# A group's score and attention products in stands of six and two, in a kernel ordered by a planner

## The chip, the cores and the metric

The kernel runs on one core of a Trainium2 chip (trn2). The metric is the device time of one execution in microseconds (us), as the median of several runs. A profile is one further execution, recorded by the hardware.

## What is computed

The input x holds 128 items of 128 x 512 floats, adj is one 128 x 128 adjacency matrix. The reference has two layers, cut here to what matters (shapes are of one item):

```python
# layer 0: gnn on adj, then layernorm over the last axis
A = adj @ x;  C = adj @ x + b[:, None]
pre = A[:, None, :] + (C - A)[:, :, None]      # C - A is b alone
x = layernorm(x + max(relu(pre), axis=-1))     # one number for each row: relu(max(A) + b)
# layer 1: masked attention with 8 heads, projection, two layernorms
q, k, v = split(x @ w_qkv, heads=8)
attn = softmax(where(adj == 0, -inf, q @ k.T * 64 ** -0.5))
o = (attn @ v) @ w_proj + b_proj
o = o + layernorm(o) * ln_gamma + ln_beta
x = layernorm(x + o)
```

All is in float32 with the accuracy of float32. A full float32 product takes TensorE several passes, so the kernel splits most operands: a number is written as a high part and a low rest, and a product is the sum of high x high, low x low and a term of the differences, each in the faster type fp32r.

## The kernel before

**Items and groups.** The 128 items are worked in 32 groups of G = 4. In a program place, the first number is the group and the second the item of the group or, for dense products, one of twelve: 0 to 3 are v of the four items, 4 to 11 are the eight slices of q and k for all four items at once.

**Steps of an item.** Each step is a small function that issues one or a few instructions.
- Layer 0: load (DMA of x), conv (adj times x on PE, full float32, L632), cmax (L643), relu, then either bn, ba, rstdx, shiftx (items 0 and 1; bn is L680 on DVE) or add0, sq0, rstd0, shift0 (items 2 and 3), and norm0 on ACT.
- Transposed x: xpl (ACT copies into 16-bit planes, L716), xrow (DMA to rowsx in memory), xcross (a transposing DMA back, xT), then xmask, xsub, xhigh, xd make the three split forms x_h, x_l, x_d.
- Dense products: dm (eight fp32r products, L817 and L818) and dd (four, L823), then main (ACT takes the first bank out of PSUM, L842) and rest (DVE adds the second, L846).
- Attention: S (scores: sixteen products, each with 64 rows of the array, L863), masked and rmax (DVE, L877 and L885), exps (ACT, eight exponentials, L902), recip and wts (DVE, L911), pln (ACT, L917), row (DMA to rows), cross (transposing DMA, eT), AV (weights times v: sixteen products, each with 64 columns of the array, L949).
- Projection: omask, osub, ohigh, od make oh, ol and od (L739, L967, L743 or L745, L749); po and pod are its products (eight and four, again L817, L818, L823; od and o are printed with the item's number); pmain and prest (DVE, L986 and L1012) take them out.
- The end of an item: res, resx, resb, reso bring in the first layer's x a second time; sq1, sm1, st1, n1a, n1b and sq2, sm2, st2, norm2 are the two layernorms; out is the last DMA.

In the last group, T (transposes on PE) and wT take the place of pln, row and cross, and S of item 3 adds the mask by four products (L857).

**The order.** The order on every engine (PE, ACT, DVE, POOL and SP, which issues nearly all DMAs) is written out: each step has a place in a table (STEADY for the middle groups, FIRST for groups 0 and 1, LAST for groups 30 and 31, SETUP for weights and constants), a group's places are shifted by g x PERIOD, all steps are sorted by place, and each engine gets its steps in that order. Places in STEADY read like microseconds; only the order that they give reaches the chip. Each engine runs in order and waits at a step whose inputs or buffer are not ready.

```python
u0 = g * PERIOD
...
at(u, single[kind], b)
...
plan.sort(key=lambda p: p[:2])
```

**Buffers.** HOMES says, for each kind of tile and each group, which numbered buffer it gets. PSUM has two pools: ps_1 with four single banks (pa of conv, pav of AV, pm and pd of dense products, pom and pod of the projection) and ps_2 with two double banks (psc of the scores; pp and ppo, where a product that TWO marks with 1 keeps both its banks together). So TWO's rows dense and po say which products take a double bank. Its rows d and h say which of xd and od (first four entries for x, next four for o) and of xhigh and ohigh run on POOL: a 1 puts the difference on POOL and not on DVE, the high part on POOL and not on ACT.

In the middle groups PE meets the special products of a group in this order, with dense products between the brackets: [AV of items 2 and 1 of the group before, S of 0 and 1], [S of 2 and 3, AV of 3 of the group before], [AV of 0]. Such a run without a dense product in it is called a stand here. The last one stands between conv products.

Of the kernel before, what the change touches and what calls it, by code (L numbers as in the profile page):

```python
# [8 lines left out]
FP = mybir.dt.float32  # L9
# [18 lines left out]
PERIOD = 55.65721  # L28
STEADY = {
    'load': [-84.387, -101.525, -92.757, -104.895],  # L30
    'conv': [-75.113, -75.979, -71.238, -73.133],
    'cmax': [-74.046, -74.912, -70.171, -71.594],
    'relu': [-73.282, None, -69.407],
    'bn': [-79.685, -90.339],
    'ba': [-78.963, -87.311],
    'rstdx': [-71.500],
    'shiftx': [-67.749],
    'add0': [None, None, -69.067, -62.343],
    'sq0': [None, None, -68.228, -60.929],
    'rstd0': [None, None, -60.228],  # L40
    'shift0': [None, None, -20.160],
    'norm0': [-66.552, -60.223, -55.338, -56.756],
    'xpl': [-65.714, -57.708, -54.441, -46.941],
    'xrow': [-64.641, -56.635, -53.368, -45.398],
    'xcross': [-61.931, -52.928, -48.082, -41.718],
    'xmask': [-54.951, -43.405, -41.164, -36.407],
    'xsub': [-48.801, -42.437, -37.819, -35.400],
    'xhigh': [-46.997, -35.315, -37.063, -35.835],
    'xd': [-26.327, -29.608, -22.523, -17.793],
    'dm': [4.837, 11.201, 6.655, 16.122, -27.595, -10.169, -22.140, -32.141, -33.960, -23.959, -25.777, -30.323],  # L50
    'dd': [9.383, 10.292, 20.788, 27.152, -12.896, -6.532, -8.350, -5.623, -4.714, -16.490, -7.441, -11.987],
    'main': [7.711, 13.218, 9.668, 20.862, -11.380, -7.877, -11.865, -20.987, -31.942, -21.472, -23.760, -26.046],
    'rest': [10.516, 14.823, 28.292, 38.461, -10.247, -5.049, -3.873, -4.461, -2.608, -11.977, -6.331, -9.059],
    'S': [0.000, 0.997, 13.110, 14.107],
    'masked': [1.644, 5.106, 15.417, 27.161],
    'rmax': [3.380, 8.064, 24.101, 29.327],
    'exps': [4.623, 15.506, 26.003, 35.155],
    'recip': [10.406, 20.865, 29.217, 43.570],
    'wts': [11.110, 22.861, 30.453, 44.268],
    'pln': [13.703, 24.200, 32.382, 51.803],  # L60
    'row': [20.837, 26.467, 34.304, 55.119],
    'cross': [24.197, 29.995, 47.113, 59.806],
    'AV': [37.158, 54.685, 53.762, 70.756],
    'omask': [41.739, 55.758, 58.432, 77.236],
    'osub': [42.962, 56.693, 64.847, 80.884],
    'ohigh': [46.552, 56.528, 63.853, 84.748],
    'od': [47.794, 58.991, 74.103, 86.254],
    'po': [51.853, 58.675, 73.718, 96.599],
    'pod': [57.646, 64.130, 75.536, 100.236],
    'pmain': [60.163, 63.121, 81.492, 101.655],  # L70
    'prest': [61.894, 65.455, 82.210, 102.843],
    'res': [41.103, 53.159, 76.024, 78.628],
    'resx': [52.598, 58.118, 78.904, 82.973],
    'resb': [53.844, 60.258, 80.456, 101.811],
    'reso': [62.664, 71.516, 83.739, 104.286],
    'sq1': [66.881, 66.175, 85.753, 103.922],
    'sm1': [66.639, 71.226, 88.501, 103.613],
    'st1': [68.723, 67.062, 90.348, 105.534],
    'n1a': [69.485, 72.830, 94.712, 105.600],
    'n1b': [77.841, 75.237, 95.973, 108.029],  # L80
    'sq2': [78.635, 93.900, 96.767, 110.927],
    'sm2': [90.058, 96.472, 97.864, 110.751],
    'st2': [94.366, 98.154, 99.952, 125.624],
    'norm2': [95.548, 105.334, 102.729, 130.428],
    'out': [97.230, 106.460, 109.286, 132.611],
# [3 lines left out]
        'load': [-311.682, -309.097, -309.092, -289.177],  # L89
        'conv': [-301.956, -285.978, -284.699, -252.846],  # L90
        'cmax': [-276.686, -268.417, -252.229, -243.444],
        'relu': [-275.480, -258.624, -245.414, -236.373],
        'bn': [-298.400, -272.353, -260.336, -251.012],
        'ba': [-276.256, -271.589, -254.792, -248.969],
        'rstdx': [-272.599, -269.091, -248.273, -238.464],
        'shiftx': [-269.130, -253.340, -240.209, -232.976],
        'norm0': [-266.978, -249.667, -237.355, -228.662],
        'tx': [-266.046, -245.978, -230.203, -224.006],
        'copy': [-248.555, -225.163],
        'pv': [-226.671, -221.380],  # L100
        'keep': [-210.841, -209.446],
        'xmask': [-237.451, -231.282, -228.825, -220.542],
        'xsub': [-232.807, -226.381, -226.376, -184.540],
        'xhigh': [-235.047, -224.785, -216.680, -210.529],
        'xd': [-232.210, -205.597, -206.130, -125.910],
        'dm': [None, None, 8.596, 7.614, -27.333, -7.643, -16.082, -37.145, -46.738, -6.339, -11.225, -36.934],
        'dd': [None, None, 7.519, 13.277, -25.364, -7.365, -10.388, -25.470, -13.330, -4.235, -16.812, -26.914],
        'main': [None, None, 9.424, 14.292, -8.119, -5.070, -13.376, -26.832, -30.312, -2.548, -8.551, -26.673],
        'rest': [None, None, 11.233, 35.409, -6.802, -0.906, -5.599, -18.911, -0.865, 0.048, -7.653, -11.149],
        'S': [0.071, 3.526, 11.673, 10.965],  # L110
        'masked': [4.362, 7.230, 17.266, 20.450],
        'rmax': [4.711, 7.375, 18.562, 27.402],
        'exps': [6.391, 14.172, 25.847, 36.857],
        'recip': [12.522, 19.013, 30.495, 40.437],
        'wts': [13.400, 26.323, 35.020, 43.252],
        'pln': [14.511, 33.217, 37.332, 48.065],
        'row': [24.078, 40.304, 45.297, 48.373],
        'cross': [31.686, 41.648, 45.892, 58.796],
        'AV': [38.517, 48.815, 50.261, 70.407],
        'omask': [43.804, 51.125, 58.512, 81.275],  # L120
        'osub': [44.138, 53.164, 60.683, 86.080],
        'ohigh': [45.476, 55.853, 65.956, 87.153],
        'od': [52.512, 60.084, 71.048, 87.521],
        'po': [48.135, 56.775, 71.054, 93.215],
        'pod': [54.003, 61.222, 76.700, 97.775],
        'pmain': [55.811, 59.410, 82.388, 98.578],
        'prest': [56.183, 64.180, 82.945, 101.590],
        'res': [46.370, 42.491, 71.387, 79.013],
        'resx': [63.966, 47.589, 79.420, 100.786],
        'resb': [70.459, 70.785, 81.534, 105.046],  # L130
        'reso': [70.474, 72.568, 90.218, 105.110],
        'sq1': [63.146, 65.537, 87.020, 104.749],
        'sm1': [69.929, 71.912, 90.063, 105.360],
        'st1': [72.212, 72.233, 94.751, 105.573],
        'n1a': [78.126, 76.071, 96.130, 106.436],
        'n1b': [82.298, 76.869, 96.351, 108.235],
        'sq2': [82.739, 79.519, 97.605, 111.944],
        'sm2': [87.842, 82.457, 97.845, 117.109],
        'st2': [90.386, 87.300, 99.888, 120.030],
        'norm2': [95.187, 93.693, 107.047, 122.559],  # L140
        'out': [99.205, 96.285, 112.844, 132.585],
    },
    {
        'load': [-131.325, -146.629, -109.252, -117.493],
        'conv': [-103.575, -126.260, -90.173, -103.104],
        'cmax': [-94.745, -125.823, -83.341, -89.398],
        'relu': [-80.440, None, -75.846],
        'bn': [-106.480, -139.224],
        'ba': [-99.960, -134.812],
        'rstdx': [-91.047],  # L150
        'shiftx': [-79.188],
        'add0': [None, None, -74.243, -74.248],
        'sq0': [None, None, -69.318, -69.504],
        'rstd0': [None, None, -68.606],
        'shift0': [None, None, 14.252],
        'norm0': [-78.560, -74.678, -62.455, -54.484],
        'xpl': [-77.724, -72.376, -61.942, -52.495],
        'xrow': [-75.147, -66.114, -52.002, -51.491],
        'xcross': [-52.007, -55.219, -51.696, -50.648],
        'xmask': [-51.097, -51.522, -47.743, -46.741],  # L160
        'xsub': [-47.766, -48.031, -45.293, -45.741],
        'xhigh': [-44.210, -49.814, -42.689, -41.925],
# [31 lines left out]
        'n1b': [80.034, 71.944, 89.870, 107.555],  # L194
        'sq2': [83.515, 87.175, 100.626, 112.358],
        'sm2': [85.095, 77.407, 91.265, 112.382],
        'st2': [89.764, 89.887, 102.645, 129.724],
        'norm2': [94.880, 93.286, 102.685, 130.269],
        'out': [99.098, 100.886, 102.826, 130.308],
    },  # L200
# [951 lines left out]
```

## Time and profile before

| what | us |
|---|---|
| median of three runs | 1847.24 (1846.62 to 1847.33) |
| the profiled execution, its own time | 1842.58 |
| its span, from the first instruction to the last | 1840.6 |
| PE busy | 1804.2 |
| DVE busy | 1548.9 |
| ACT busy | 1541.5 |
| POOL busy | 1311.4 |

The clock that PE was granted is 0.996 of full over the span. A page of the profile gives busy time by engine first, then groups of instructions with their mean duration and what they waited for. In a line of the order of time the columns are: start, duration, engine, line of the kernel, operation, output<-inputs, count of merged instructions, and in brackets the engine's idle time before it and what ended it. A line of the waits has: who waited, for whom, total, times, longest. A line of busy time by stretch has: the stretch, its length, busy time and count of PE, weight loads, DVE, ACT and POOL, granted clock, share of DMA time, GB/s.

### The profile page before, as it was taken

Reading aid. Unit: us, or ns where it says so; the run is one execution under the profiler, and the core shown is the slowest. Engines: PE = TensorE matmul, PEld = TensorE weight load, DVE = VectorE, ACT = ScalarE, POOL = GpSimd, SP = SyncE. Lnnn points to the kernel's source line nnn. Section 1 sums busy time; section 2 is a strip of 40 time slices with the busy share of each in tenths; the row PEclk is TensorE's granted clock in tenths of the full one; section 3 lists DMA queues with packets and bytes.
Section 4 is the critical chain, followed back from the end, with each engine's and each line's share of the span. In section 5 each row is a group of like instructions: output and inputs, shape, how many; then the busy total and the mean of one; then the engine's idle time right before and its main releaser. Section 6 shows DMA issues by size and latency. Waiting matters only on the chain. (4 is left out here: it accounts for less than half of the span.)

```text
span 1840.6 us, 32730 instructions
## 1 busy us (share of the span) xinstructions
PE 1804.2 (98%) x10541; PEld 1426.1 (77%) x10541; DVE 1548.9 (84%) x2584; ACT 1541.5 (84%) x3927; POOL 1311.4 (71%) x1935
## 2 busy tenths in 40 slices
PE   8999999999999999999999999999999999999995
PEld 5777777778777788777787777787777787777874
DVE  7988888888888888888888888888888888788877
ACT  6988888888888888888888888888888888878865
POOL 4277787677777777777676877776877777667768
PEclk9999999999999999999999999999999999999998
DMA  5556665666575676565676656675656665656641
GB/s 150 173 149 182 170 171 162 163 179 183 150 185 165 158 191 171 157 175 160 175 183 166 170 169 162 174 184 161 180 162 159 185 184 149 178 144 178 155 126 46
DMA packets 486139, 302.91 MB, mean 165 GB/s; under 512 B 399440, under 2 KB 403664, under 8 KB 485968
## 3 DMA queue, kind: packets, MB, share of 16 engines
q1 hardware_dynamic: 485104, 299.70, 60.6%
q8 instruction: 84, 1.38, 0.3%
q10 hardware_dynamic: 864, 1.12, 0.2%
q14 instruction: 87, 0.71, 0.1%
HBM read 72.16 MB, written 131.07 MB: 110 GB/s over the span
## 5 line engine op out<-in xcount | busy, mean ns | idle before, releaser
L902 ACT ACTIVATE e<-e,nmax 128x128 f32<-128x128 f32 x1016 | 393.1, 390 | 34.9 <-DVE nmax L885 34.8
L917 ACT COPY planes<-e 128x2048 uint16<-128x2048 uint16 x124 | 234.9, 1894 | 41.7 <-DMA rows<-planes 20.4
L1018 ACT ACTIVATE square<-o,sum 128x512 bf16<-128x512 f32 x256 | 183.6, 717 | 88.0 <-DVE o L1012 87.0
L1002 POOL TENSOR_SCALAR xb<-xb,sum 128x512 f32<-128x512 f32 x128 | 109.5, 855 | 194.9 <-DMA xb<-in_x_dram 185.7
L1024 POOL TENSOR_TENSOR sum<-sum,mhalf 128x1 f32<-128x1 f32 (+1 forms) x287 | 195.5, 681 | 23.9
L1009 POOL TENSOR_TENSOR xb<-xb,o 128x512 f32<-128x512 f32 x125 | 173.4, 1387 | 35.9 <-DVE o L1012 33.7
L902 ACT ACTIVATION_READ_ACCUMULATOR e<-e,nmax 128x1 f32 x1016 | 191.9, 189 | 0.0
L911 DVE TENSOR_TENSOR e<-e,sums 128x1024 f32<-128x1024 f32 x128 | 175.9, 1375 | 0.1
L1005 POOL TENSOR_TENSOR xb<-xb,beta_sb 128x512 f32<-128x512 f32 x128 | 167.4, 1308 | 4.9
L716 ACT COPY xplanes<-xt 128x1024 uint16<-128x1024 uint16 x124 | 129.1, 1041 | 41.4 <-DMA rowsx<-xplanes 40.5
L1023 POOL TENSOR_SCALAR sum<-sum 128x1 f32<-128x1 f32 (+1 forms) x287 | 122.4, 427 | 56.3 <-ACT square L1018 36.9
L877 DVE SCALAR_TENSOR_TENSOR e<-psc,mask 128x1024 f32<-128x1024 f32 x127 | 154.4, 1216 | 1.3 <-PE psc L863 1.3
L885 DVE TENSOR_REDUCE nmax<-e 128x8 f32<-128x1024 f32 x127 | 151.7, 1195 | 0.1
L643 DVE TENSOR_REDUCE rm<-pa 128x1 f32<-128x512 f32 x128 | 87.7, 688 | 68.0 <-PE pa L632 66.4
L739 DVE TENSOR_SCALAR oxh<-pav 128x512 int32<-128x512 int32 x128 | 87.2, 681 | 64.5 <-PE pav L949 62.8
L949 PEld LDWEIGHTS pav<-eT,v 128*64 128x64 f32 x2048 | 109.8, 137 | 38.1 <-issue 16.4
L863 PEld LDWEIGHTS psc<-qkT 64*128 64x128 f32 x2048 | 119.5, 188 | 18.5 <-issue 17.0
L749 POOL TENSOR_TENSOR x_d<-x_h,x_l 128x512 fp32r<-128x512 f32 x97 | 128.9, 1332 | 6.2 <-DVE x_l L755 6.2
L949 PE MATMUL pav<-eT,v 128*64 128x128 f32 x2048 | 133.2, 277 | 0.0
L863 PE MATMUL psc<-qkT 64*128 64x128 f32 x2048 | 132.3, 279 | 0.6 <-DVE v L846 0.4
L632 PE MATMUL pa<-xt,adjT 128*128 128x512 f32 x256 | 131.1, 615 | 0.5 <-DVE adjT L561 0.4
L1039 DVE SCALAR_TENSOR_TENSOR o<-o,sum,gamma_sb 128x512 f32<-128x512 f32 x128 | 99.4, 778 | 31.0 <-POOL xb L1009 23.8
(4288 smaller groups left out, 5533.3 us busy)
## 6 DMA issues: line engine op xcount, KB each, us to landing
rows<-planes SPq DMA_DIRECT2D x124, 512.0 KB, 3.8
xt<-in_x_dram SPq DMA_DIRECT2D x128, 256.0 KB, 3.6
xb<-in_x_dram SPq DMA_DIRECT2D x128, 256.0 KB, 3.0
out_dram<-o SPq DMA_DIRECT2D x128, 256.0 KB, 3.2
rowsx<-xplanes SPq DMA_DIRECT2D x124, 256.0 KB, 2.8
wraw<-in_L_gnn_w_qkv_dram SPq DMA_DIRECT2D x8, 256.0 KB, 3.6
xT<-rowsx SPq DMA_TRANSPOSE x124, 3.6
eT<-rows SPq DMA_TRANSPOSE x124, 4.4
```

The costliest lines, as they stand in the source:

```text
L632: nc.tensor.matmul(pa[b], adjT, xs[b], start=True, stop=True)
L863: nc.tensor.matmul(psc[:, s, hp, :], qkT[hs, hp, i, :], qkT[hs, KC + hp, i, :], start=not with_mask, stop=not with_mask or hp == HP - 1,)
L877: nc.vector.scalar_tensor_tensor(es[b], pscs.pop(b).rearrange("p s a m -> p (s a) m"), scale, mask_b, op0=ALU.mult, op1=ALU.add,)
L885: nc.vector.tensor_reduce(nmaxs[b], es[b], AX.X, ALU.max, negate=True)
L902: nc.scalar.activation(es[b][:, j, :], src[:, j, :], AF.Exp, bias=nmax[:, j : j + 1], scale=by, accum_out=sums[b][:, j : j + 1],)
L911: nc.vector.tensor_tensor(es[b], es[b], sums.pop(b)[:, :, None].to_broadcast([P, H, P]), op=ALU.mult,)
L917: nc.scalar.copy(pl, es.pop(b).rearrange("p h m -> p (h m)").bitcast(U16).rearrange("p (m s) -> p s m", s=2),)
L949: nc.tensor.matmul(pavs[b][s * HD : (s + 1) * HD, hp, :], v[:, h * HD : (h + 1) * HD], eT[:, s * HP + hp, :], start=True, stop=True,)
L1005: nc.gpsimd.tensor_tensor(xbs[b], xbs[b], beta_sb, op=ALU.add)
L1009: engine.tensor_tensor(xbs[b], xbs[b], os[b], op=ALU.add)
L1018: nc.scalar.activation(square, src, AF.Square, bias=s[:, 0:1], scale=-float(D), accum_out=s[:, 1:2],)
L1024: nc.gpsimd.tensor_tensor(s, s, mhalf[:, :n], op=ALU.pow)
```

## The change

All tables are replaced: PERIOD, STEADY, FIRST, LAST, SETUP, TWO and HOMES. In the middle groups, PE's special products now stand as [S of items 2 and 0, AV of items 1 and 0 of the group before, S of 1 and 3] and [AV of 2 and 3 of the group before]; the four conv products stand singly between dense ones. In FIRST, LAST and SETUP many places are thousands, with the order in them alone of effect. Each step still occurs as often as before. TWO moves one high part and one difference of a group to another engine and changes which products use a double bank. There is a new branch in po and pmain (one full float32 product in place of the split ones in the last group) with two new steps, lp and ocopy; TWO's row plain is all zeros and no table holds places for lp or ocopy.

```diff
-PERIOD = 55.65721
+PERIOD = 55.29520
 STEADY = {
-    'load': [-84.387, -101.525, -92.757, -104.895],
+    'load': [-87.861, -88.331, -108.598, -116.436],
...
-    'bn': [-79.685, -90.339],
+    'bn': [-75.588, -84.750],
...
-    'xrow': [-64.641, -56.635, -53.368, -45.398],
-    'xcross': [-61.931, -52.928, -48.082, -41.718],
+    'xrow': [-68.575, -61.581, -56.570, -52.833],
+    'xcross': [-63.957, -56.130, -50.263, -41.238],
...
+    'dm': [-2.906, 7.680, 4.876, 14.911, -28.277, -11.089, -13.817, -31.005, -15.635, -26.459, -32.823, -23.775],
+    'dd': [11.317, 12.226, 20.653, 26.109, -17.453, -11.998, -6.543, -18.363, -9.271, -16.544, -7.452, -8.362],
+    'main': [8.036, 20.173, 9.041, 17.942, -26.260, -9.072, -11.799, -25.069, -12.689, -20.790, -30.806, -20.305],
...
-    'S': [0.000, 0.997, 13.110, 14.107],
-    'masked': [1.644, 5.106, 15.417, 27.161],
+    'S': [0.000, 2.887, -0.997, 3.884],
+    'masked': [1.332, 5.529, 0.201, 14.546],
...
-    'row': [20.837, 26.467, 34.304, 55.119],
-    'cross': [24.197, 29.995, 47.113, 59.806],
-    'AV': [37.158, 54.685, 53.762, 70.756],
+    'row': [15.477, 39.515, 52.228, 59.088],
+    'cross': [23.799, 44.363, 61.747, 64.017],
+    'AV': [57.210, 56.287, 72.115, 73.038],
...
 LAST = {
     -2: {
-        'load': [-107.823, -91.695, -103.440, -73.255],
+        'load': [-91.734, -89.477, -107.242, -114.634],
...
-        'bn': [-105.550, -89.567],
+        'bn': [-84.588, -84.468],
...
     -1: {
-        'AV': [43.664, 48.635, 62.710, 73.994],
+        'AV': [2284.230, 2274.397, 2965.116, 2626.927],
...
 TWO = {
+    'plain': [0, 0, 0, 0],
     'bn': [1, 0],
-    'd': [1, 1, 1, 0, 0, 1, 0, 1],
-    'dense': [1, 0, 0, 0, 1, 0, 1, 0, 0, 0, 0, 0],
-    'h': [1, 0, 0, 0, 0, 1, 0, 0],
-    'po': [0, 0, 1, 0],
+    'd': [0, 1, 0, 1, 1, 1, 1, 1],
+    'dense': [0, 1, 0, 0, 0, 0, 0, 0, 0, 0, 0, 0],
+    'h': [0, 0, 0, 0, 1, 0, 0, 0],
+    'po': [1, 0, 1, 0],
...
+    def plain(b):
+        return bool(TWO["plain"][b % G]) and b >= B - G
...
     def po(b, two):
-        product(("o", b), two)
+        if plain(b):
...
+        else:
+            product(("o", b), two)
```

## The prediction

> **What bounds the kernel now.** I read the page's first part, then busy time by stretch, then the waits of PE, then PE's order of time around the attention products. A difference under 0.2% (3.7 us) can't be told from none here.
>
> ```profile
> PE 1804.2 (98%) x10541; PEld 1426.1 (77%) x10541; DVE 1548.9 (84%) x2584; ACT 1541.5 (84%) x3927; POOL 1311.4 (71%) x1935
> ```
> ```profile
> 500.00:1500.00 1000.00, 999.37 (x5864) 797.18 (x5860) 844.79 (x1418) 860.25 (x2194) 733.54 (x1076) 1.00 0.64 171
> ...
> 1770.00:1841.00 71.00, 49.30 (x336) 37.66 (x331) 54.27 (x89) 40.54 (x120) 57.50 (x87) 0.92 0.21 64
> ```
> ```profile
> PE pd_('o', 109)_17866 L823 <- DVE o L1012: 2.5, 1, 2.5
> PE pd_(31, 3)_20003 L823 <- DVE o L986: 2.4, 1, 2.4
> PE pm_('o', 127)_20090 L818 <- DVE w_l L967: 2.3, 1, 2.3
> PE pd_('o', 127)_20104 L823 <- POOL w_d L749: 2.1, 1, 2.1
> PE pp_(31, 0)_19602 L823 <- ACT v L842: 2.0, 1, 2.0
> ```
> In the middle PE never rests; the others have 14% (ACT) to 27% (POOL) spare. Order matters there only through what PE pays between products. The first score products of neighbouring groups start 55.58 us apart in 17 of the 25 pairs from group 3 to 28; the other eight add 4.2 us in all. The end is different: PE is idle 21.7 of the last 71 us, and waits after 1690 add to 11.0 us.
>
> What PE pays between products is read from start times:
>
> ```profile
> 928.63 0.39 PE L818 MATMUL pm_('o', 60)_10246<-p_l,ol 128*128 128x512 f32 x1
> 928.95 1.97 PE L949 MATMUL pav<-eT,v 128*64 128x128 f32 x32
> 930.84 2.06 PE L863 MATMUL psc<-qkT 64*128 64x128 f32 x32
> 932.83 1.20 PE L823 MATMUL pd_('o', 60)_10322<-p_d,od 128*128 128x512 f32 x4
> 933.86 0.39 PE L817 MATMUL pm_('o', 61)_10334<-p_h,oh 128*128 128x512 f32 x1
> ```
> ```profile
> 910.55 1.88 PE L632 MATMUL pa<-xt,adjT 128*128 128x512 f32 x4
> 912.36 1.09 PE L949 MATMUL pav<-eT,v 128*64 128x128 f32 x16
> 913.38 1.12 PE L632 MATMUL pa<-xt,adjT 128*128 128x512 f32 x2
> 913.94 1.50 PE L823 MATMUL pd_(16, 9)_10106<-x_d,w_d 128*128 128x512 f32 x4
> 915.28 1.02 PE L632 MATMUL pa<-xt,adjT 128*128 128x512 f32 x2
> ```
> A dense product takes 0.227 us from start to start, a pair of AV products 0.109 and a pair of score products 0.112, in a run of their own kind. First fence: 0.32 into AV instead of 0.23 (0.09 too much); two AV batches 1.89 instead of 16 x 0.109 = 1.75 (0.14); two score batches 1.99 instead of 1.79 (0.20); the four dense ones after them 1.03 instead of 0.91 (0.12). So **prices**: 0.21 for a stand (in and out of dense work), 0.20 for each block of scores, 0.15 for each block of AV, whatever their length. Check on the second fence: from 910.55 to 915.28 are 4.73; six passes of conv (0.4285), one AV batch (0.875) and four dense ones (0.907) make 4.35. 0.38 against 0.21 + 0.15.
>
> **What the Trainium skill says.** "TensorEngine Tiling (Array Packing)", Key Properties: changing the tiling mode, not just the tile, drains TensorE. Scores are 64x128, AV 128x64, the rest 128x128. The trace agrees: each change costs 0.09 to 0.2 us. "TensorE: Matmul & The Clock Gate", Architectural detail: ScalarE's and VectorE's queues are strict FIFO, so what waits holds all behind it; the wait at 1607 (below) is that. The same page, Part 1: idleness throttles PE's clock until it has been busy for a window of some 3.4 us. After 2.5 us of idleness at 1608 four products took 1.98 us from first start to last end, against 1.07 in the middle: agrees, a stall costs more than itself.
>
> **The change, part by part.** The order of every engine follows from sorting the tables by place; I sorted both.
>
> *Stands.* Before, per group: [A2 A1 S0 S1], [S2 S3 A3], [A0] between conv products: 3 stands, 2 score blocks, 3 AV blocks: 3 x 0.21 + 2 x 0.20 + 3 x 0.15 = 1.48. After: [S2 S0 A1 A0 S1 S3], [A2 A3]: 2 stands, 2 and 2 blocks: 1.12. So -0.36 a group. Over the program I count 99 stands, 64 score and 97 AV blocks before (48.1 us), 76, 68 and 69 after (39.9): the ends, where the order splits stands, give some back. -8.2 us, all on PE, which sets the end: taken in full. A conv product now stands alone four times a group, not in two runs; entering from dense work starts it 0.232 after instead of 0.227, so +0.007 x 29 more entries = +0.2. Sum **-8.0**. The mode changes inside the new stand (S to AV to S) both occur in the old ones, so no price is unseen.
>
> *Work moved between engines.* Per group one high part (L743, 1.50 on POOL) goes to ACT (L745, 0.62); one difference (L749) goes from DVE (0.68) to POOL (1.30). POOL -0.2, ACT +0.6, DVE -0.7, of 55: hidden under PE while ACT keeps its 14%; if that cover is gone, +0.6 a group. The number of products, exponentials and DMAs is the same.
>
> *DMA leads.* SP issues in order and holds when a source isn't ready; its waits before are mostly transposes issued before their rows landed. Leads of rows to eT were 3.4, 3.5, 12.8, 4.7 us for a median landing of 3.8; now 8.3, 4.9, 9.5, 4.9. rowsx to xT: 2.7 at the least before, 4.6 now (landing 2.8). Better, but AV stands at least 6.7 us after the issue of its eT in both (landing 4.4): no PE time, 0. One lead is tighter: bn of item 1 stands 3.6 us after its load (11.2 before) and a load lands in 3.6 (1 in 20 over 4.8). What is queued behind bn on DVE is the rest step of v; then qkT sums wait, then PE. The table leaves DVE 0.8 us after it. 0 to +0.3 a group; taken: within the next item.
>
> *PSUM slots.* Three of the twelve dense products of a group took a wide slot (dm4 among them), now one; the output products take two instead of one. So 34 single-bank tiles a group pass four banks, 32 before. By the places, the narrowest reuse was 0.4 to 0.7 us before; now dd5 starts 0.69 after main8 starts on the same bank, dm5 0.71 after main6, dd11 0.71 after main5, and main takes 0.58. So 0.04 of margin. ACT's run from main4 to main8 (13.6 us) has almost no gap. Bounds: -4.2 (all present stray waits go, as the DMA leads are better) to +0.8 a group (22). Taken: 0, new small waits for the old ones. S1 and S3 reuse the wide slots of S2 and S0: 1.2 to 1.4 us left after masked; 13 us before; no wait.
>
> *The wait at 1607.* DVE's order of time shows a bn (L680) that waited 3.4 us for its load; prest queued behind it, PE's pd waited for that, then ran slow; that group took 60.4 instead of 55.6: 4.8 us. In the old LAST table this bn stood 2.1 us behind its load. In the new one the leads of bn there are 7.1, 5.0, 12.5 and 22.6. What could be late next is another transfer; I take **-3.5**, bounds -4.8 and +1.
>
> *The last two groups.* 11.0 us of waits after 1690. Old order ends AV, o, q for items 2 and 3 with nothing else left for PE. The new one does T for all, keeps o and q of item 30.3 for the gap after them, and puts both last AV ahead of three output products in a row (8.2 us). Counting by hand after q31.1: DVE needs prest, n1b, osub, omask, reso, n1a, n1b (5.0), ACT a square (0.9), POOL st2 (1.0) before od31.3 (1.3): 8.2, while PE has one AV, o31.0, q31.0, o31.3 (5.8): a wait of 2.4 stays. T31.2 and o31.3 come out even. With 3 to 4 unseen, 6 of 11: -5, bounds -9 and +4. The chain behind the last product (12.1 us now: 1828.5 to 1840.6) gets a POOL step more in it: +0.7. Sum **-4.3**.
>
> *The start.* Waits up to 200 us are some 5 us before (0.2 to 0.7 each). New order: two weight conversions stand ahead of those that d0.8 needs, by hand +1; nothing says that the rest is better. **+1.5**, bounds -4 and +5.
>
> plain is all zeros and no table has places for lp or ocopy: none of that runs, 0.
>
> Sum: -8.0 + 0 - 3.5 - 4.3 + 1.5 = **-14.3**. The profiled execution took 1842.58 (span 1840.6 and 2.0 around it), 4.7 less than the median of 1847.24; against it 1828.3, as a median 1833.
>
> **Rivals.** (1) *Switches alone*: the ends don't gain. For: hand counting sees few queues at once. -7 to -9: 1839. (2) *The ends gain fully*: -9 there, stray waits gone: -21, 1826. (3) *Slower: ACT releases banks late.* At the places with 0.04 us left (dd5, dm5, dd11), PE waits in every group. For: no gap in ACT's run, ACT +0.6; against: ACT's measured steps fit the places within 0.02 us. At 0.8 a group, 28 groups: +22, so 1855; it decides from 14.3 / 28 = 0.5 a group. (4) *No change*: PE's switches are saved, but a wait before the next product takes them up each group: 1847.
>
> **How the numbers follow.** Forecast 0.52 (1828 to 1838), rival 1 0.20, rival 2 0.10, rival 4 0.07, rival 3 0.11. Faster by over 0.2%: 0.82; same 0.07; slower 0.11. The range of 8 in 10 goes from 1824 (inside rival 2) to 1846 (rival 1 with its bounds, the edge of rival 4); the slower case is left out.
>
> **What would show it.** Right: groups 55.2 to 55.3 apart; six-batch stand about 5.9 us from first score to first dense product; no wait of 2 us near 1600; under 8 us of PE waits after 1680. Wrong: PE waits for ACT (L842) at pd or pm of 5, 6, 8, 11 in many groups, groups over 55.6 apart, or DVE waits for xt before L680 in each group.

## The result, and the profile after

The change makes no difference that can be measured: 1847.55 us after against 1847.14 before, medians of twelve runs each, ratio 1.0002 (95% interval 0.9993 to 1.0011). The forecast was 1833, and its range ended at 1846. The profiled execution took 1845.31 us (span 1843.2), 2.7 more than that of before.

First the lines that answer to those of before. The page's busy times of the kernel after:

```profile
PE 1805.7 (98%) x10541; PEld 1426.9 (77%) x10541; DVE 1535.2 (83%) x2551; ACT 1556.9 (84%) x3958; POOL 1293.9 (70%) x1937
```

Busy time by stretch, the middle and the end:

```profile
500.00:1500.00 1000.00, 999.42 (x5890) 796.79 (x5889) 836.38 (x1400) 869.17 (x2213) 718.92 (x1077) 1.00 0.65 170
1770.00:1843.20 73.20, 49.72 (x310) 37.81 (x308) 49.15 (x83) 38.84 (x116) 56.75 (x83) 0.84 0.19 58
```

PE's waits, the longest of the whole kernel:

```profile
PE adjT_ps L554 <- DMA adj_sb<-in_adj_dram: 4.1, 1, 4.1
PE pm_('o', 127)_20094 L813 <- ACT w_h L741: 3.9, 1, 3.9
PE pd_('o', 127)_20104 L819 <- POOL w_d L745: 2.5, 1, 2.5
```

And the new stand of six batches in PE's order of time:

```profile
928.33 0.39 PE L814 MATMUL pm_(16, 0)_10225<-w_l,x_l 128*128 128x512 f32 x1
928.64 2.06 PE L859 MATMUL psc<-qkT 64*128 64x128 f32 x32
930.63 1.97 PE L945 MATMUL pav<-eT,v 128*64 128x128 f32 x32
932.53 2.06 PE L859 MATMUL psc<-qkT 64*128 64x128 f32 x32
934.51 0.50 PE L813 MATMUL pm_(16, 2)_10332<-w_h,x_h 128*128 128x512 f32 x1
934.85 0.40 PE L814 MATMUL pm_(16, 2)_10332<-w_l,x_l 128*128 128x512 f32 x1
```

The engines moved as forecast (ACT up, DVE and POOL down), the 2.5 us wait at the `pd_` of output 109 is gone, and two waits in the last group are the only ones over 1 us that PE has left after the start. The stand takes 5.87 us from first score to first dense product, as forecast. Yet the span is no shorter. Where it went is seen by cutting the span at the first score product of a group:

| stretch, us | before | after | difference |
|---|---|---|---|
| start to group 3 | 205.6 | 203.8 | -1.8 |
| group 3 to group 28 | 1393.7 | 1394.0 | +0.3 |
| group 28 to group 31 | 171.6 | 168.4 | -3.2 |
| group 31 to the end | 69.7 | 77.0 | +7.3 |

In the 25 pairs of the second row the undisturbed step went from 55.58 to 55.75; before, stray waits raised the mean of all 25 to 55.75 too, and after there are almost none (mean 55.76). So two things have to be explained: the step that did not fall to 55.2, and the last 7.3 us.

### The profile page after: what moved, and what is told of

Its sections match the earlier page's. It is cut to its first block, busy times and chain, and to the rows that moved or that the text cites. A ratio compares the mean times of both kernels' runs of the same rounds, so it can differ in the third digit from the quotient of the medians.

```text
span 1843.2 us, 32644 instructions
## 1 busy us (share of the span) xinstructions
PE 1805.7 (98%) x10541; PEld 1426.9 (77%) x10541; DVE 1535.2 (83%) x2551; ACT 1556.9 (84%) x3958; POOL 1293.9 (70%) x1937
## 5 line engine op out<-in xcount | busy, mean ns | idle before, releaser
L745 POOL TENSOR_TENSOR od<-oh,ol 128x512 fp32r<-128x512 f32 x124 | 165.0, 1331 | 133.8 <-DVE ol L963 78.0
L1051 POOL TENSOR_TENSOR sum<-sum,mhalf 128x1 f32<-128x1 f32 (+1 forms) x287 | 213.6, 744 | 23.9
L1036 POOL TENSOR_TENSOR xb<-xb,o 128x512 f32<-128x512 f32 x125 | 163.4, 1307 | 53.4 <-DVE o L1039 50.8
L907 DVE TENSOR_TENSOR e<-e,sums 128x1024 f32<-128x1024 f32 x128 | 161.4, 1261 | 1.1
L739 POOL TENSOR_SCALAR oh<-oxh 128x512 fp32r<-128x512 f32 x31 | 64.0, 2065 | 113.4 <-DVE oxh L735 27.3
L1029 POOL TENSOR_SCALAR xb<-xb,sum 128x512 f32<-128x512 f32 x128 | 119.2, 931 | 17.6 <-DMA xb<-in_x_dram 17.4
L945 PE MATMUL pav<-eT,v 128*64 128x128 f32 x2048 | 127.5, 276 | 1.8 <-DVE e L873 0.9
L1039 DVE SCALAR_TENSOR_TENSOR o<-o,sum,xb 128x512 f32<-128x512 f32 x128 | 100.6, 787 | 20.8 <-POOL sum L1051 15.5
L1087 ACT ACTIVATE o<-o,sum 128x512 f32<-128x512 f32 x128 | 103.2, 807 | 12.3 <-POOL sum L1083 12.2
```

What stands on the lines that cost most here:

```text
L745: engine.tensor_tensor(d, h.bitcast(FP), l.bitcast(FP), op=ALU.subtract)
L907: nc.vector.tensor_tensor(es[b], es[b], sums.pop(b)[:, :, None].to_broadcast([P, H, P]), op=ALU.mult,)
L945: nc.tensor.matmul(pavs[b][s * HD : (s + 1) * HD, hp, :], v[:, h * HD : (h + 1) * HD], eT[:, s * HP + hp, :], start=True, stop=True,)
L1036: engine.tensor_tensor(xbs[b], xbs[b], os[b], op=ALU.add)
L1051: nc.gpsimd.tensor_tensor(s, s, mhalf[:, :n], op=ALU.pow)
```

## The experiments

In the names of steps and items, dd5 is dd of dense product 5, main8 is main of dense product 8, sq21 is sq2 of item 1, and 31.3 is item 3 of group 31 (127 in the names of the profile). Each ratio is to the kernel before on the same chip. "Step" and "end" are read from one profile of each kernel: "step" is the median distance of first scores in the 25 pairs, and "end" the time from the first score of group 31 to the end. Kernels with nearly the same step and end as after have ratios up to 0.0016 apart from it (e4, e6, e9), and the end varies from 76.2 to 77.1 among kernels with one and the same last group (after, e1, e2, e3). What lies under that is not read.

| run | ratio (95%) | step | end |
|---|---|---|---|
| after | 1.0002 (0.9993 to 1.0011) | 55.75 | 77.0 |
| e1_two_scratch | 0.9978 (0.9972 to 0.9985) | 55.51 | 77.1 |
| e2_interleave | 0.9981 (0.9974 to 0.9987) | 55.52 | 76.2 |
| e3_main8 | 0.9976 (0.9969 to 0.9982) | 55.52 | 76.2 |
| e5_scratch_before | 0.9992 (0.9984 to 1.0001) | 55.58 | 69.6 |
| e7_conv | one run | 55.62 | 69.7 |
| e4_tail | 1.0014 (1.0007 to 1.0021) | 55.76 | 77.2 |
| e12_after_o | 1.0005 (0.9997 to 1.0013) | 55.76 | 76.2 |
| e9_pool_relief | 1.0018 (1.0010 to 1.0026) | 55.75 | 78.4 |
| e6_chain | 1.0017 (1.0008 to 1.0025) | 55.75 | 76.5 |
| e8_all | 0.9976 (0.9966 to 0.9986) | 55.49 | 76.6 |
| e10_all_relief | 0.9966 (0.9952 to 0.9980) | 55.49 | 74.7 |
| e11_o_buffers | 0.9952 (0.9940 to 0.9965) | 55.49 | 73.3 |
| e15_last_sums | 0.9955 (0.9941 to 0.9969) | 55.49 | 71.3 |

### The middle groups: three squares in a row on ACT

In the trace of after, PE loses 0.31 us in each group at dd5. Neither the busy time nor the waits show it, since the products overlap and the record of the one ahead ends only 0.04 us before; it is read from start times. dd5 should start 0.227 after the product ahead of it and starts 0.43 after it (and its second product another 0.11 late). PE's order of time:

```profile
972.78 0.39 PE L814 MATMUL pm_(17, 6)_10724<-x_l,w_l 128*128 128x512 f32 x1
973.21 1.20 PE L819 MATMUL pd_(17, 5)_10745<-x_d,w_d 128*128 128x512 f32 x4
974.24 0.39 PE L813 MATMUL pm_(17, 5)_10757<-x_h,w_h 128*128 128x512 f32 x1
```

Its bank comes free when ACT's main8 (the move of `pm_(17, 8)`) is done. ACT's order of time ahead of it:

```profile
965.14 0.73 ACT L1045 ACTIVATE square<-o,sum 128x512 bf16<-128x512 f32 x1
965.76 0.21 ACT L1045 ACTIVATION_READ_ACCUMULATOR square<-o,sum 128x1 f32 x1
966.00 0.72 ACT L1045 ACTIVATE square<-o,sum 128x512 bf16<-128x512 f32 x1
966.63 0.19 ACT L1045 ACTIVATION_READ_ACCUMULATOR square<-o,sum 128x1 f32 x1
966.85 0.72 ACT L1045 ACTIVATE square<-xt,sum 128x512 bf16<-128x512 f32 x1
...
967.57 1.88 ACT L913 COPY planes<-e 128x2048 uint16<-128x2048 uint16 x1
...
971.86 0.81 ACT L700 ACTIVATE xt<-xt,sum 128x512 f32<-128x512 f32 x1
972.58 0.57 ACT L838 ACTIVATE qkT<-pm_(17, 8)_10710 128x512 f32<-128x512 f32 x1
```

The last square has 0.72 to the next operation. The first two have 0.86 and 0.85. All three write the same tile, `square`, which nobody reads: only their accumulated sums are used. Two times 0.14 make 0.28 of the 0.31 us. The theory: a square that writes the tile of the square just ahead of it can't overlap with it, and this makes main8 and dd5 late.

**e1_two_scratch** gives the squares two tiles in turn, of a one-byte type:

```diff
-    square = const.tile([P, D], mybir.dt.bfloat16, name="square")
+    scratch = [const.tile([P, D], mybir.dt.float8e4, name=f"square{i}") for i in range(2)]
...
     def squares(src, s):
+        scratch.reverse()
         nc.scalar.activation(
-            square, src, AF.Square, bias=s[:, 0:1], scale=-float(D), accum_out=s[:, 1:2],
+            scratch[0], src, AF.Square, saturate=False, bias=s[:, 0:1], scale=-float(D), accum_out=s[:, 1:2],
```

> The kernel after, with two one-byte scratch tiles used in turn for the unused output of the squares, in place of one two-byte tile. Theory (in each middle group three squares stand in a row on ACT, each starts 0.85 us after the one before instead of 0.71, main8 comes 0.28 us late, PE waits 0.31 us at dd5; the cause is that they all write one tile): the step falls to 0.71, the wait at dd5 goes, groups 55.75 to about 55.45 apart, 28 groups, -8 us: 1839. Rival (the 0.14 us belongs to two squares in a row, whatever they write): step stays 0.85, no change, 1847.

ACT's order of time at the same three squares:

```profile
964.44 0.72 ACT L1045 ACTIVATE square<-o,sum 128x512 fp8e4<-128x512 f32 x1
965.05 0.20 ACT L1045 ACTIVATION_READ_ACCUMULATOR square<-o,sum 128x1 f32 x1
965.14 0.72 ACT L1045 ACTIVATE square<-o,sum 128x512 fp8e4<-128x512 f32 x1
965.75 0.20 ACT L1045 ACTIVATION_READ_ACCUMULATOR square<-o,sum 128x1 f32 x1
965.85 0.72 ACT L1045 ACTIVATE square<-xt,sum 128x512 fp8e4<-128x512 f32 x1
```

and PE's at dd5:

```profile
972.07 0.39 PE L814 MATMUL pm_(17, 6)_10725<-x_l,w_l 128*128 128x512 f32 x1
972.30 1.09 PE L819 MATMUL pd_(17, 5)_10746<-x_d,w_d 128*128 128x512 f32 x4
973.22 0.43 PE L813 MATMUL pm_(17, 5)_10758<-x_h,w_h 128*128 128x512 f32 x1
```

The squares follow each other in 0.70 and 0.71, each still 0.72 long, and dd5 starts 0.23 after its predecessor. The step falls by 0.24 to 55.51. The Trainium skill ("ScalarE: Activation LUTs", What ACT_TABLE_LOAD costs) states that ACTIVATEs back to back overlap by some 93 ns. Here the second square starts 0.11 before the first one's accumulator read ends (965.14 against 965.25), close to that figure; in after it starts 0.03 behind that end (966.00 against 965.97). So the page holds for two tiles, and the overlap is lost on one.

e1 changes the type of the tile too. Against the type as the cause speaks a pair that keeps its step in e1: a square that reads what the relu just ahead of it has written.

```profile
950.92 0.71 ACT L648 ACTIVATE xt<-xt,rm 128x512 f32<-128x512 f32 x1
951.54 0.19 ACT L648 ACTIVATION_READ_ACCUMULATOR xt<-xt,rm 128x1 f32 x1
951.76 0.72 ACT L1045 ACTIVATE square<-xt,sum 128x512 fp8e4<-128x512 f32 x1
```

It starts 0.03 behind the end of the read, 0.84 after the relu, with a one-byte output (0.83 in after, 0.85 in before). So what costs is that an operation depends on the one just ahead of it. Writing into one tile is not enough: the eight exponentials of an item write different parts of one tile, and in after they start 0.386 apart though each takes 0.39 and its accumulator read ends later still.

**e2_interleave** keeps the one tile and parts the squares: sq21, norm22, sq10, pln1, sq02.

```diff
-    'sq0': [None, None, -73.703, -87.671],
+    'sq0': [None, None, -71.590, -87.671],
-    'norm2': [110.625, 102.524, 149.986, 131.962],
+    'norm2': [110.625, 102.524, 146.700, 131.962],
```

> The kernel after, with ACT's order in the middle groups sq21, norm22, sq10, pln1, sq02 in place of sq21, sq10, sq02, pln1, norm22: the same work ahead of main8, no two squares in a row. Theory (any two squares in a row cost 0.14 more, and this makes main8 and dd5 late): wait at dd5 gone, groups about 55.45 apart, 1839. Rival (ACT is simply too full ahead of main8, or the bank is late for another reason): wait stays, 1847. Rival (the wait is taken up by the next one in line, dd11 or dm5): wait at dd5 gone, groups still over 55.65 apart, 1845 or more.

Step 55.52. The same work in another order does what the second tile did, so it is not the load of ACT, and the gain needs no one-byte type.

**e3_main8** leaves the squares slow and puts main8 one place ahead (`'main'`, ninth place: -12.689 to -13.420).

> The kernel after, with main8 ahead of norm01 on ACT in the middle groups (one place of one step: main8 comes 0.72 us sooner, norm01 0.48 later). Theory (dd5 waits for the bank of main8 alone): wait at dd5 gone although the squares still take 0.85 each; groups about 55.45 apart, 1839; what stays of main5's lateness stays at dd11 (0.06). Rival (another bank or the later norm01 takes the time back): 1845 or more.

Step 55.52 too. 0.06 stays at dd11, and 0.06 appears at dm5, whose bank main6 frees: the two other places that the prediction had named.

**e5_scratch_before** is the control: e1's edit on the kernel before.

> The kernel before, with the same two one-byte scratch tiles in turn. Theory (a square after a square costs 0.14 us in both kernels, but in the old order no bank that PE waits for comes behind such a pair): the squares step 0.71, groups stay 55.58 apart, no change (within 0.1%). Rival (ACT's time as such holds the kernel, or the one-byte tile itself is what helped): before gains as after did, 0.3 to 0.4%.

The one pair of squares in a row that a group of the old order has falls from 0.85 to 0.72, and the step stays 55.58. A slow pair costs only where a bank comes behind it. In all three cures about 0.24 us a group came back where the theory said 0.30: the rest shows as small excesses at dd5 and dm5, and the 0.06 at dd11 stayed.

### The middle groups: conv alone

**e7_conv** puts one conv of the kernel before between dense products, as the new order has them (`'conv'`, second place: -75.979 to -77.804).

> The kernel before with the conv of item 1 alone between two dense products (ahead of dm6) in the middle groups, in place of next to that of item 0: one more lone conv a group. Theory (dense products that follow a lone conv run 0.235 to 0.240 apart in place of 0.227, 0.04 us for each exit): undisturbed groups 55.62 to 55.63 apart in place of 55.58. Rival (it is the place in the new order, not the lone conv): 55.58.

Step 55.62: 0.04 for one more lone conv. It is not the entry, which the prediction priced (0.232 less 0.227 is 0.005; its sum has 0.007), but the exit: behind the first of the next eight dense products, seven steps take 1.62 us in place of 1.59. Single ones lie between 0.224 and 0.236, so the 0.235 to 0.240 of the expectation is too much for their mean, which is 0.232. In after, the four exits of a group lose 0.011, 0.034, 0.034 and 0.022 in these steps; in before, two exits lose 0.023 and 0.022. That makes 0.06 more a group, and 0.08 with the first step, which takes 0.637 to 0.639 behind three of the four in place of 0.633.

### The last group: several limits of the same length

In after, PE waits 6.4 us for the output products of 31.3, and DVE's order of time shows another wait beside it:

```profile
1822.65 0.69 DVE L1013 SCALAR_TENSOR_TENSOR o<-pm_('o', 127)_20094,bias_sb 128x512 f32<-128x512 f32 x1 [4.46 <-DMA out_dram<-o]
1823.45 0.69 DVE L1039 SCALAR_TENSOR_TENSOR o<-pd_('o', 127)_20104,o 128x512 f32<-128x512 f32 x1
...
1827.79 0.69 DVE L1013 SCALAR_TENSOR_TENSOR o<-pp_('o', 126)_20110,bias_sb 128x512 f32<-128x512 f32 x1 [3.65 <-issue]
```

**e4_tail** takes PE's waits away; in the last group alone:

```diff
-        'omask': [2595.470, 2280.785, 3162.865, 2988.471],
-        'osub': [2820.893, 2434.855, 3429.992, 3159.684],
-        'ohigh': [2750.204, 2451.872, 3286.893, 3316.324],
-        'od': [3039.224, 2892.794, 3633.889, 3616.193],
+        'omask': [2595.470, 2280.785, 3005.000, 2988.471],
+        'osub': [2820.893, 2434.855, 3015.000, 2995.000],
+        'ohigh': [2750.204, 2451.872, 3010.000, 3000.000],
+        'od': [3039.224, 2892.794, 3050.000, 3043.000],
...
-        'resx': [3336.479, 2694.938, 3829.281, 3414.706],
+        'resx': [3560.000, 2694.938, 3829.281, 3565.000],
```

> The kernel after, in the last group alone: the high part, the low part and the difference of the output of items 31.3 and 31.2 come as soon as their AV is there (ohigh ahead of the square of 31.1 on ACT, osub and omask ahead of n1a30.3 on DVE, od ahead of resb31.1 on POOL), and two resx behind st230.3 on POOL. Theory (PE's 6.4 us of waits ahead of po31.3 and pod31.3, and the throttled clock after them, come from these steps queued behind steps that wait): PE's last product ends 8 to 10 us sooner, the end comes 5 to 8 us sooner, 1841. Rival (the chain of norms of the last items on DVE and POOL sets the end, PE's waits are only on the way): PE ends sooner but the end moves less than 2 us, 1846.

PE's last product ends 51.0 us after the first score of group 31 (61.5 in after, 57.6 before), 10.5 sooner, and the end does not move (77.2). So neither PE's waits nor its lower clock in the last stretch (0.84, before 0.92) set the end by themselves. DVE's order of time shows what it waits for:

```profile
1828.45 0.69 DVE L1013 SCALAR_TENSOR_TENSOR o<-pm_('o', 127)_20094,bias_sb 128x512 f32<-128x512 f32 x1 [5.44 <-DMA out_dram<-o]
```

The rival, that the end would hardly move, was right. There are three o buffers; 31.3 has that of 31.1 and waits until its out has landed.

**e12_after_o** takes this wait away instead: in the kernel after, 31.0, 31.2 and 31.3 get tiles that held exponentials.

```diff
     def pmain(b):
-        os[b] = tile_at(work, "o", [P, D], FP, f"o_{b}", "o", *divmod(b, G))
+        spare = {B - 4: 0, B - 2: 1, B - 1: 2}.get(b)
+        if spare is None:
+            os[b] = tile_at(work, "o", [P, D], FP, f"o_{b}", "o", *divmod(b, G))
+        else:
+            os[b] = work.tile([P, H, P], FP, tag=f"e_{spare}", bufs=1, name=f"o_{b}").rearrange("p h m -> p (h m)")[:, :D]
```

> The kernel after with those three tiles and nothing else. Theory (in the new order PE's late products, POOL's full queue and the o buffers each hold the last items until about the same time, so one alone gives nothing): the wait for a DMA at L1013 goes, the end comes less than 1 us sooner. Rival (the o buffers alone set the end): 3 to 5 us sooner, ratio 0.998.

DVE's waits in the last group of this kernel (lines of pmain and prest are 4 higher):

```profile
DVE o L1017 <- PE pp_('o', 126)_20110 L819: 3.6, 1, 3.6
...
DVE o L1043 <- PE pd_('o', 127)_20104 L819: 2.3, 1, 2.3
```

The first of these stood in after too (the 3.65 above). The second, and 1.0 us at `pm_` of 127, are new: 3.3 us of waiting for PE in place of the 4.46 for the buffer. From the first score of group 31 on, pmain31.3 starts 3.5 us sooner (53.0 against 56.5), prest31.3 only 1.3 (56.0 against 57.3), and the end comes 0.8 sooner.

**e9_pool_relief** takes five steps (6.3 us of work) from POOL to DVE, two of them (od31.0 and od31.2) at earlier places, and changes nothing else.

```diff
-        'od': [3039.224, 2892.794, 3633.889, 3616.193],
+        'od': [2985.000, 2892.794, 3435.000, 3616.193],
...
-        nc.gpsimd.tensor_tensor(xbs[b], xbs[b], beta_sb, op=ALU.add)
+        engine = nc.vector if b >= B - 2 else nc.gpsimd
+        engine.tensor_tensor(xbs[b], xbs[b], beta_sb, op=ALU.add)
...
-                    at(u, f, b, bool(two[i]))
+                    at(u, f, b, bool(two[i]) and not (last and kind == "od" and i in (0, 2)))
...
-    'tail_vector': [0, 1, 1, 1],
+    'tail_vector': [1, 1, 1, 1],
```

> The kernel after, with five steps of the last group moved from POOL to DVE and nothing else: od31.0, od31.2, resb31.2, resb31.3 and reso31.0 (6.3 us of POOL's busy time, 3.4 of DVE's; DVE waits some 17 us after 1766). Theory (POOL, which the new tables give all differences of the outputs, is busy without a gap from 1785 to 1829 and sets the end through the sums that DVE and ACT wait for): the end comes 3 to 6 us sooner, 1842 to 1844 where after takes 1847; POOL gets gaps before 1830. Rival (the end is a chain of dependent steps of the last items on three engines, with POOL full only beside it): under 1.5 us.

Nothing gained (78.4): POOL now stands still for 8.2 us, from 57.8 us after the first score of group 31 on, but the two waits of PE and the one of DVE for the buffer are all still there. **e6_chain** joins e4's edits with an earlier end of item 30.3 (sq2, sm2, st2, norm2, out; st2 of 30.2 is earlier too, od31.2 and pmain31.2 later) and an exchange of the o buffers of 31.2 and 31.3; **e8_all** adds e2's edit and norm01 behind main6 (`'norm0'`, second place: -68.696 to -66.580). In e6, the lines of group 30, and those of `'o'` in HOMES:

```diff
-        'sq2': [2493.237, 1760.632, 2976.836, 3254.808],
-        'sm2': [1921.825, 1828.948, 3018.160, 3473.653],
-        'st2': [2528.768, 2033.360, 3135.653, 3542.995],
-        'norm2': [2639.507, 2052.978, 3248.824, 3833.127],
-        'out': [2968.875, 2348.409, 3425.425, 3981.636],
+        'sq2': [2493.237, 1760.632, 2976.836, 3180.000],
+        'sm2': [1921.825, 1828.948, 3018.160, 3288.300],
+        'st2': [2528.768, 2033.360, 3101.300, 3289.300],
+        'norm2': [2639.507, 2052.978, 3248.824, 3355.000],
+        'out': [2968.875, 2348.409, 3425.425, 3430.000],
...
-        '11000000000000000000000000000002',
-        '00212121212121212121212121212121',
+        '11000000000000000000000000000001',
+        '00212121212121212121212121212122',
```

> The kernel after with the edits of e4_tail and more in the last two groups: item 30.3 finishes sooner (its second square, st2, norm2 and out ahead of those of 31.1; st230.2 and st131.1 ahead of od31.2 on POOL), pmain31.2 behind n1a31.0 on DVE, and items 31.2 and 31.3 exchange their o buffers, so that 31.3 takes the one of 30.3. Theory (the end is set by DVE's pmain, which waits for an o buffer until the out DMA of an earlier item has landed; three buffers for the last items): the wait for a DMA at L1013 falls from 4.5 to under 1.5, the end comes 2.5 to 5 us sooner than after: 1842 to 1844 where after takes 1847. Rival (the sum of DVE's and POOL's work after the last AV sets the end, whatever waits): under 1 us.

> All together on the kernel after: squares interleaved as in e2_interleave, norm01 behind main8 and main6 on ACT in the middle groups, and the last two groups of e6_chain. Theory (both losses are separate and add): waits at dd5 and dm5 gone, groups 55.40 to 55.50 apart, the tail 2.5 to 5 us shorter: 1836 to 1839 where before takes 1847. Rival (a wait that is not seen yet takes over when ACT is out of the way): groups over 55.5 apart, 1841 or more.

The wait for a DMA fell to 2.3 in all (longest 2.0), but in its place DVE waits 7.6 us for POOL's sums (3.7 in after), 3.9 at once, and PE 3.0 for a difference that POOL makes; the end is at 76.5 and 76.6, where e6's theory had it 2.5 to 5 us sooner. In e8 the steady half came (step 55.49), the tail half did not. From there the limits go one by one: POOL's relief on top (**e10_all_relief**), then e12's o tiles, with pmain31.2 and prest31.2 ahead of n1a31.0 and res31.2 earlier (**e11_o_buffers**; `'prest'`, third place: 4140.759 to 3912.000), then the first sums of 31.3 and 31.2 ahead of the second ones of 31.0 (**e15_last_sums**):

> The kernel e8_all with the same five steps on DVE. Theory (e6_chain took waits away from PE and DVE but left POOL's sum of work; with it eased they count): the time from the first score of group 31 to the end falls from 76.5 to about 70, 1833 where before takes 1847 (ratio 0.993 to 0.995). Rival (nothing to gain in the tail in this order): 1838, ratio 0.997 to 0.998 as e8_all.

> The kernel e10_all_relief with the outputs of items 31.0, 31.2 and 31.3 in tiles that held the exponentials (free once T is done), in place of the three o buffers; with it pmain31.2 and prest31.2 ahead of n1a31.0 on DVE and res31.2 ahead of the outs on SP. Theory (with PE's and POOL's waits gone, what is left between PE's last product at 51.5 us after the first score of group 31 and the end at 74.8 is pmain waiting until an out DMA has landed, and what is queued behind it): no wait for a DMA at L1013, end 68 to 71 us after that score; about 1833 where before takes 1846, ratio 0.993 to 0.995. Rival (the dependent steps of the last items, 13 us from pmain31.2 to the end, and POOL's queue keep it): 74 us, ratio 0.996 to 0.997.

```diff
-        'sq1': [3766.697, 3103.563, 4364.182, 4151.003],
-        'sm1': [3983.741, 3230.880, 4380.221, 4279.414],
-        'st1': [3972.922, 3228.819, 4501.812, 4281.125],
+        'sq1': [3766.697, 3103.563, 4152.000, 4151.003],
+        'sm1': [3983.741, 3230.880, 4157.000, 4155.000],
+        'st1': [3972.922, 3228.819, 4158.000, 4156.000],
...
```

> The kernel e11_o_buffers with the first sums of items 31.3 and 31.2 (sq1, sm1, st1, then n1a and n1b) ahead of the second sums of 31.0 on ACT, POOL and DVE, and resx31.2 next to the other resx. Theory (in e11_o_buffers prest of 31.2 is done at 1817, but st1 of 31.3 stands on POOL behind st2 of 31.0 and runs at 1825; the rest of the loss is this order): first score of group 31 to the end falls from 73.3 to 68 to 70, ratio 0.992 to 0.994 to before. Rival (the chain of dependent steps from prest to out takes this time in any order): 72.5 to 74, ratio 0.995.

The end comes at 74.7, 73.3 and 71.3. The same steps that gave nothing singly (POOL: none; o tiles: 0.8, no more than the end varies by itself) give 1.8 and 1.4 once the others are away. Each came with small shifts of order beside it, so the shares are not exact; and they are smaller than the theories of e10 (to about 70) and e11 (to 68 to 71) had them, e11 lying next to its rival. e15 landed between its two expectations: the order of the last sums was 2.0 of the open 3.6 us. From the first score of group 29, which leaves out where the two orders cut group 30 from 31, before takes 180.9 us to the end, after 186.8 and e15 181.7. So all but 0.8 us of the loss at the end lies in these queues and buffers, as one profile of each shows it.

e15_last_sums is faster than both kernels: 1834.65 us where before took 1843.44 on that chip. Its ratio can't be told from e11's, so the last 2.0 us rest on the two profiles alone.

## Why the prediction was wrong

- **What bounds the kernel: right in the middle, wrong at the end.** Between 500 and 1500 PE is busy 999.4 of 1000 us in both kernels. In the last group it is one of several bounds.
- **Stands, -0.36 a group: right.** From 928.33 to 934.85 are 6.52 us. Three times 16 pairs (2 x 1.79 and 1.74) and two dense steps of 0.227 make 5.78, so the stand costs 0.74; 0.21 + 2 x 0.20 + 0.15 is 0.76. Summed over both stands, 1.09 after against 1.43 before: -0.34.
- **Conv entries, +0.2: mis-sized.** The exits were left out: 0.06 to 0.08 a group, 1.7 to 2.2 us over 28.
- **Work moved between engines, 0: right.** ACT kept its spare time; what failed was its order, not its load (e2).
- **DMA leads and bn1, 0: right.** Of fifty bn between 200 and 1600 one waits for its load, 0.2 us.
- **PSUM slots, taken 0: this is the step that failed.** It named dd5, dm5 and dd11 with 0.04 us of margin, and then trusted that ACT's steps fit their places within 0.02. (0.69 less 0.58 is 0.11; 0.04 comes out only if some 0.06 pass between the end of main8 and the start of dd5, as they do in after, from 973.15 to 973.21. The prediction doesn't name these 0.06.) The steps do fit, except for a square behind a square: 0.85 in place of 0.71. The old trace held one such pair a group, the new table three. Measured: dd5 0.31 and dd11 0.06, 0.37 a group, which is inside the bounds (-0.15 to 0.8), against 0.5 from which rival 3 decides. The lower bound came true as well: the stray waits went, 0.17 a group on average.
- **Sum of a group:** -0.34 + 0.31 + 0.06 + 0.08 + 0.03 (the products after the scores) is +0.14, where +0.17 was measured, from 55.58 to 55.75; 0.03 has no place in this sum. The mechanism in the middle is that of rival 3 (ACT releases a bank late, PE waits at dd5 and dd11 in every group), the size is that of rival 4, which had a chance of 0.07.
- **The wait at 1607, -3.5: right in kind, too large.** The wait is gone, but that pair of groups went only from 60.39 to 58.58, 1.8 less, with two more conv passes (0.86) and a wait of 0.7 for ACT in it.
- **The last two groups, -4.3: this failed too.** The hand count gave PE's wait at od31.3 (2.4, measured 2.5) but had po31.3 come out even. It waited 3.9, because ohigh31.3 stands on ACT behind squares that wait for DVE. More than that, it took PE's waits for the time to the end; e4 took them away and the end stayed. The chain after PE's last product, priced at +0.7, grew from 12.1 to 15.5.
- **The start, +1.5: not seen.** It was -1.8 in this profile; in the other runs with the new start the first score of group 3 came at 204.4 to 206.9, with the old start at 204.9 to 206.3.

Against the forecast of -14.3 the middle row of the table missed by 9.3 (25 x 0.36 = 9.0 forecast, +0.3 measured), and what comes from group 28 on by about 11; the start came out 3.3 better than forecast. Of the signs that the prediction set out, the stand of 5.9 us and the quiet at 1600 came true; groups over 55.6 apart, a sign of being wrong, came true as well, and PE's waits after 1680 were 8.9 us, not under 8.

## What to carry to other kernels

When an order is packed until margins are a few hundredths of a microsecond, price each step with its neighbour in the new order, not by its mean in the old one: look in the trace for every pair that will stand together, for a step that reads what the one ahead of it wrote, and for outputs that nobody reads but that share a tile. In a tail, take one limit away at a time before believing in any: where several engines end together, removing PE's waits, a buffer or a queue alone may show nothing, and the gain shows only when all are gone. An order that holds one item's products back as filler may also hold back its buffers and its sums: when item 30.3 ended earlier and 31.3 took its buffer, the waits for a buffer fell from 5.8 us (e4) to 2.3 (e6).

## What the runs showed of the hardware

In these kernels an ACT operation that depends on the one just ahead of it loses the overlap with it. Two squares that write the same output start 0.85 us apart, in both kernels, and 0.70 to 0.72 with two outputs in turn (e1, e5). A square that reads what the relu ahead of it wrote starts 0.83 to 0.85 after it, with one output or two. Exponentials that write different parts of one tile keep their overlap (0.386 apart). A conv, a full float32 product, that stands alone among fp32r products costs about 0.04 us behind it: in e7 the step of a group went from 55.58 to 55.62.
